# Two engines share the sums of a pairwise-tanh attention by a running tally, and last sums stay in PSUM

## The chip, the cores and the metric

The kernel runs on one core of a Trainium2 chip. The core's engines run side by side, each from its own queue, in order: TensorE (PE in the profile, its weight loads PEld), VectorE (DVE), ScalarE (ACT), GpSimd (POOL) and SyncE (SP, which issues the transfers here). Each waits on semaphores for what others made. The metric is the device time of one execution in microseconds; the median of three executions is compared. All arithmetic is fp32, and TensorE runs each fp32 matmul as two instructions.

## The reference

Two layers work on 8 images of 128 channels by 36 x 36 positions. Layer 0 normalises groups of channels, runs 3 x 3 and 1 x 1 convolutions and a softmax attention, and adds the result to x. Layer 1 takes the 1296 positions as tokens of 128 channels. Its attention scores are a sum over channels of a tanh:

```python
q = jnp.einsum('bld,ed->ble', x, Wq) + bq
k = jnp.einsum('bld,ed->ble', x, Wk) + bk
t = jnp.tanh(q[:, :, None, :] + k[:, None, :, :])
scores = jnp.einsum('bijd,d->bij', t, w) + bw[0]
attn = jax.nn.softmax(scores, axis=-1)
return jnp.einsum('bij,bjd->bid', attn, x)
```

That is 1296 x 1296 x 128 tanh values an image. After it comes a mixture of 64 experts: each expert takes its 8 best tokens of an image, weighted by a softmax over the tokens, runs a two-layer network on their weighted mean, and adds the result back to the tokens.

## The kernel before

**The scores.** The kernel never forms the tanh itself. Over a common denominator, a group of channels' tanh terms is a ratio of two sums of products of exponentials, one factor of which depends on the query alone and one on the key alone. So a numerator and a denominator are each a matmul of query features (`qf`) and key features (`kf`). A unit is one key tile (128 keys, or 16 in the last of 11 tiles) against one query chunk of 432 tokens; there are 8 images x 3 chunks x 11 tiles = 264 units. A unit has 12 slots (3 for the short last tile), 2952 in all. In each slot:

- `numerators(p)`: TensorE makes two 128 x 432 numerators into two tiles `n` of a PSUM pool of four (`ps_n`), which all other work's PSUM tiles (`aux`) take turns in too.
- `denominators(p + LAG)`, three slots ahead: TensorE makes two denominators into `d` (another pool of two), ScalarE takes Ln of them (L815), and after every second slot Exp of the negated logs (L818), which leaves reciprocals in `lq`.
- `terms(p, ns)`: VectorE multiplies each numerator by its reciprocal, and the two products join the unit's running sum.

The sum is kept in two places. In most slots the products go to an SBUF tile `rp` (pool `rpp`, three buffers, L846) and GpSimd adds both at once to `accp` (L851, L853). In the slots named by `DVE_PAIRS = (2, 5, 8, 11)`, VectorE multiplies in place in PSUM (L840) and adds each product to `accd` itself (L842; the first such slot of a unit writes `accd` by its first product, L835 to L837). At a unit's end `sums(u)` has GpSimd add the halves of `accp` and then `accd` (L860, L863), and seven slots later `exps` takes the exponential on ScalarE (L878).

**All the other work** is written as generators that stop at `yield` and are resumed between slots: `normal` (group normalisation), `conv_keys` and `layer0` (convolutions and attention of the next image), `tokens` (token normalisation of the next image), `keys`, `query_block` (query features: an Exp on ScalarE and a product by GpSimd, L594), `attend` and `gating`. `take_turns` resumes those that want no TensorE; `matmul_turn` resumes those that do, while a balance holds: each slot adds `PACE = 370` columns, and each background matmul takes its columns plus 20 off it. So the order on each engine is fixed when the program is built, by counts of slots and columns and not by time. Before the loop (up to 193 us) image 0 is prepared by the same generators without slots between; behind it (from 6240 us) the last attends, the last gating and the experts run.

**`attend`** forms the weighted token sums: 12 tiles of 108 queries an image, 96 in all. For each, two groups of matmuls over the key tiles end in two PSUM tiles `pa`. VectorE copies the first to SBUF (`sums`, L625), adds the second to it in SBUF (L628), takes the reciprocal of the last column (L630), multiplies, adds the tokens `t2` (L631) and takes statistics (L635, L636). Where a chunk of 432 is finished, the four tiles follow one another in the slots of about one and a third units.

**Layer 0's attention** forms, per chunk, ten exponentials `e`, their running total `tot` on GpSimd (L374), five pairs of matmuls `pa` that VectorE adds up in `ax` (L395, L397), then the matmul `pt` that sums `tot` over the keys, Ln and Exp of it on ScalarE (`ri`, L405, L406), and the product `ax * ri` (L412), both in SBUF.

Of the kernel before, what the change touches and what calls it, by code (L numbers as in the profile page):

```python
# [57 lines left out]
DVE_PAIRS = (2, 5, 8, 11)  # L58
# [6 lines left out]
def kernel(  # L65
# [55 lines left out]
    with ExitStack() as loop, ExitStack() as score:  # L121
# [110 lines left out]

        behind = [0]
# [9 lines left out]
        def conv_turns(taps, rows, y0, x0, width, dst):  # L243
            r0, nr = rows
            for t0 in range(0, 9, 2):
# [11 lines left out]
                if t0 == 0:  # L257
                    nc.vector.tensor_copy(dst, ps)
                else:
                    nc.vector.tensor_add(dst, ps, dst)  # L260
# [9 lines left out]
        def normal(b):  # L270
# [7 lines left out]
            for c in range(NCH):  # L278
                nc.vector.bn_stats(st[:, c, :], r[:, c * CH : (c + 1) * CH])
                yield step()  # L280
            mv = small.tile([C, 2], F32, tag="gn_mv", name="gn_mv")
            nc.vector.bn_aggr(mv, st)
# [5 lines left out]
            nc.vector.tensor_copy(gm, pm[:, :1])  # L288
            dev = small.tile([C, 1], F32, tag="dev", name="dev")
            nc.vector.tensor_sub(dev, mv[:, 0:1], gm)  # L290
            nc.vector.scalar_tensor_tensor(dev, dev, dev, mv[:, 1:2], ALU.mult, ALU.add)
# [10 lines left out]
            nc.gpsimd.tensor_scalar(wxn, wx_s, rs, None, ALU.mult)  # L302
# [5 lines left out]
            nc.vector.tensor_sub(bxn, bx_s, pb[:, :1])  # L308
            yield matmuls(1)
            for c in range(NCH):  # L310
# [3 lines left out]
                nc.vector.tensor_scalar(  # L314
# [14 lines left out]
        def layer0(b):  # L329
# [16 lines left out]
            for g in range(0, NDT, 4):  # L346
# [7 lines left out]
                nc.vector.tensor_copy(  # L354
# [3 lines left out]
                for j in range(full, len(some)):  # L358
                    n = some[j][1]
                    nc.vector.tensor_copy(vw[:n, g + j, :], tp[:n, j * C : (j + 1) * C])  # L360
                yield matmuls()
            hp = big_tile("hpre")[:, :N]
            for c in range(NCH):
# [7 lines left out]
                def total(j):  # L371
                    n = DTILES[j][1]
                    of = ex[0] if j == 1 else tot
                    nc.gpsimd.tensor_add(tot[:n], of[:n], ex[j][:n])  # L374
# [11 lines left out]
                ax = chunk_tile("ax0")  # L386
                for j0 in range(0, NDT, 2):
                    pa = aux("pa0")
                    for j in (j0, j0 + 1):
                        n = DTILES[j][1]  # L390
                        bmm(pa[:, :CH], vw[:n, j, :], ex[j][:n], start=(j == j0), stop=(j > j0))
                    yield TAKE
                    if j0 == 0:
                        total(NDT - 1)
                        nc.vector.tensor_scalar(ax, pa[:, :CH], 1.0 / D, None, ALU.mult)  # L395
                    else:
                        nc.vector.scalar_tensor_tensor(  # L397
                            ax, pa[:, :CH], 1.0 / D, ax, ALU.mult, ALU.add
                        )
                    yield matmuls()  # L400
                pt = aux("pt0")
                bmm(pt[:, :CH], ones[:DT], tot[:DT], start=True, stop=True)
                yield TAKE
                ri = chunk_tile("ri0")
                nc.scalar.activation(ri, pt[:, :CH], AF.Ln, scale=1.0 / D)  # L405
                nc.scalar.activation(ri, ri, AF.Exp, scale=-1.0)  # L406
# [742 lines left out]
```

## Time and profile before

| | |
|---|---|
| time, median of 3 runs | 6438.8 us (6434.69 to 6439.65) |
| the profiled execution: time, span | 6428.41 us, 6426.7 us |
| TensorE's mean granted clock in it | 0.966 of full speed |
| TensorE, VectorE, ScalarE, GpSimd busy | 6054.8, 4900.4, 5354.6, 4798.1 us |
| first and last VectorE product of a slot begin | 192.8 and 6236 us |
| 12 slots, ordinary unit | 23.0 us |

A row of a group reads: line, engine, operation, what it writes `<-` what it reads, shapes, count, then busy microseconds and the mean nanoseconds of one, then the engine's idle time before it and what ended that. A row of waits reads: who waited `<-` for whom, microseconds in all, how many times, the longest. TensorE's busy time counts matmuls in flight, which overlap; the idle time between them is therefore what is certainly lost, and no more than that is known from the busy share.

### The profile page before, as it was taken

What the parts mean: (1) busy time and instruction counts of PE and PEld (TensorE: products, weight loads), DVE (VectorE), ACT (ScalarE), POOL (GpSimd) and SP (SyncE); (2) the same over time, 40 slices, a digit from 0 to 9 for tenths busy, and PEclk for the clock granted to TensorE, in tenths of its full rate; (3) what the DMA queues carried; (4) which work ended last, traced back from release to release, by engine and by line L of the source; (5) the groups of instructions that cost most, each with busy time, mean ns of one, the idle gap of its engine ahead of it and who ended that gap; (6) DMA issues with size and microseconds to landing.
All of it is one profiled execution on the core that took longest, in us unless ns stands there. A gap on an engine that the chain in (4) does not pass through costs nothing.

```text
span 6426.7 us, 106771 instructions
## 1 busy us (share of the span) xinstructions
PE 6054.8 (94%) x40448; PEld 2813.9 (44%) x40448; DVE 4900.4 (76%) x9315; ACT 5354.6 (83%) x5426; POOL 4798.1 (75%) x2966
## 2 busy tenths in 40 slices
PE   8999999999999999999999999999999999999986
PEld 4444444444444444444444444444444444544432
DVE  3687778877788777888788887887778877778862
ACT  1788898888888888888888888888888888989970
POOL 3677777787777877777787787778777787888870
PEclk9999999999999999999999999999999999999997
DMA  0200011000110002100111001100011000100017
GB/s 28 66 31 23 22 63 36 30 24 27 56 46 19 24 27 68 33 26 22 44 47 38 22 23 53 43 32 25 20 63 43 23 24 27 61 26 28 24 66 253
DMA packets 155284, 265.78 MB, mean 41 GB/s; under 512 B 53712, under 2 KB 79824, under 8 KB 154768
## 3 DMA queue, kind: packets, MB, share of 16 engines
q1 hardware_dynamic: 154768, 258.95, 12.5%
q8 instruction: 318, 5.21, 0.3%
q14 instruction: 198, 1.62, 0.1%
HBM read 196.81 MB, written 61.83 MB: 40 GB/s over the span
## 4 chain that ended last, share of the span: by engine, by line
PE 67%; DVE 12%; ACT 7%; issue 7%; POOL 6%; DMA 1%; SPq 0%; POOLq 0%; DVEq 0%; ACTq 0%
PE n L793 30%; PE d L793 10%; PE pc L237 7%; PE pa L237 6%; ACT lq L815 5%; DVE n L840 3%; DVE rp L846 3%; PE s L237 3%; PE pk L237 3%; PE pq L237 2%; DVE accd L842 2%; POOL accp L853 2%; DVE t L631 1%; PE n L800 1%; POOL t L681 1%
## 5 line engine op out<-in xcount | busy, mean ns | idle before, releaser
L853 POOL TENSOR_TENSOR accp<-accp,rp 128x864 f32<-128x864 f32 x1464 | 2965.2, 2025 | 1028.0 <-DVE rp L846 975.3
L793 PE MATMUL n<-qf,kf 32*128 32x432 f32 (+1 forms) x11520 | 3239.2, 579 | 93.4 <-DVE rp L846 47.0
L815 ACT ACTIVATE lq<-d 128x864 f32<-128x864 f32 x2952 | 2552.6, 882 | 690.7 <-PE d L793 643.3
L793 PE MATMUL d<-qf,kf 32*128 32x432 f32 (+1 forms) x11520 | 2876.6, 568 | 21.2 <-ACT lq L815 16.4
L846 DVE TENSOR_TENSOR rp<-n,lq 128x432 f32<-128x432 f32 x3984 | 2202.6, 600 | 623.7 <-PE d L793 399.3
L818 ACT ACTIVATE lq<-lq 128x1728 f32<-128x1728 f32 x1488 | 2429.0, 1632 | 47.1
L793 PEld LDWEIGHTS n<-qf,kf 32*128 32x128 f32 (+1 forms) x11520 | 1167.1, 187 | 1703.4 <-DVE rp L846 586.3
L793 PEld LDWEIGHTS d<-qf,kf 32*128 32x128 f32 (+1 forms) x11520 | 1038.8, 188 | 392.2 <-issue 254.1
L840 DVE TENSOR_TENSOR n<-n,lq 128x432 f32<-128x432 f32 x1440 | 811.7, 608 | 280.1 <-PE n L793 239.2
L842 DVE TENSOR_TENSOR accd<-n,accd 128x432 f32<-128x432 f32 x1440 | 867.4, 602 | 24.7
L851 POOL TENSOR_TENSOR accp<-rp 128x864 f32<-128x864 f32 x264 | 533.8, 2022 | 221.1 <-DVE rp L846 217.5
L237 PE MATMUL pa<-xh,e 128*108 128x129 f32 x1920 | 262.6, 284 | 55.6 <-DVE rp L846 34.7
L860 POOL TENSOR_TENSOR accp<-accp 128x432 f32<-128x432 f32 x264 | 290.8, 1101 | 16.2
L237 PEld LDWEIGHTS pa<-xh,e 128*108 128x108 f32 x1920 | 223.3, 175 | 179.1 <-DVE rp L846 107.4
L594 POOL TENSOR_SCALAR qf<-qf,cs_s 128x432 f32<-128x432 f32 x192 | 262.7, 1374 | 42.0 <-ACT qf L593 42.0
L863 POOL TENSOR_TENSOR accd<-accp,accd 128x432 f32<-128x432 f32 x240 | 265.6, 1107 | 28.5 <-DVE accd L842 10.4
L237 PE MATMUL s<-q,k 128*116 128x432 f32 x480 | 229.8, 570 | 3.3 <-DVE q L260 2.1
L237 PEld LDWEIGHTS pk<-xT,a_k 128*128 128x128 f32 x1408 | 172.2, 193 | 109.8 <-DVE accd L842 27.6
L374 POOL TENSOR_TENSOR tot<-tot,e 116x432 f32<-116x432 f32 x192 | 212.0, 1104 | 6.1
L835 DVE TENSOR_TENSOR accd<-n,lq 128x432 f32<-128x432 f32 x240 | 144.9, 604 | 91.6 <-PE n L793 60.5
L381 ACT ACTIVATE e<-s 116x432 f32<-116x432 f32 x240 | 125.0, 521 | 106.6 <-PE s L237 105.5
L237 PE MATMUL pk<-xT,a_k 128*128 128x128 f32 (+1 forms) x1408 | 203.2, 288 | 2.6 <-DVE accd L842 2.3
(175 smaller groups left out, 4144.4 us busy)
## 6 DMA issues: line engine op xcount, KB each, us to landing
kf<-kd SPq DMA_DIRECT2D x240, 512.0 KB
kd<-ks SPq DMA_DIRECT2D x160, 256.0 KB
w<-in_weight_dram SPq DMA_DIRECT2D x32, 1024.0 KB
x<-in_x_dram SPq DMA_DIRECT2D x8, 648.0 KB
t<-tokd SPq DMA_DIRECT2D x96, 54.0 KB
t2d<-t2T SPq DMA_DIRECT2D x24, 216.0 KB
res<-t2d SPq DMA_DIRECT2D x8, 648.0 KB
out_dram<-res SPq DMA_DIRECT2D x8, 648.0 KB
```

Source lines behind the costliest of these rows:

```text
L237: mm(out, lhsT, rhs, **kw)
L594: nc.gpsimd.tensor_scalar(qf[:, 1, :], qf[:, 0, :], cs_s[:, q : q + 1], None, ALU.mult)
L793: mm(outs[h][:, :CH], kf[rows[h], q, :], qf_of[b, c, q][rows[h], part, :], start=True, stop=True)
L815: nc.scalar.activation(lq[:, o : o + 2, :], d[:, :, :CH], AF.Ln)
L818: nc.scalar.activation(some, some, AF.Exp, scale=-1.0)
L840: mult(ns[h], ns[h], lq[:, o + h, :])
L842: nc.vector.tensor_add(live["d"], ns[h], live["d"])
L846: mult(rp[:, h, :], ns[h], lq[:, o + h, :])
L851: nc.gpsimd.tensor_add(live["p"], live["r"], rp)
L853: nc.gpsimd.tensor_add(live["p"], live["p"], rp)
L860: nc.gpsimd.tensor_add(s[:, 0, :], s[:, 0, :], s[:, 1, :])
L863: nc.gpsimd.tensor_add(d, s[:, 0, :], d)
```

## The change

The fixed list of VectorE's slots goes. Instead two numbers, `ahead["v"]` and `ahead["g"]`, tally what has been put on VectorE and on GpSimd: a wrapper around each engine (`Tallied`) adds, for each instruction it issues, the columns of what it writes times a factor (1 for VectorE, 1.85 for GpSimd) plus a start (60 or 30). After each slot both are lowered by `SLOT = 1550`, not below 0. A slot's sum goes to VectorE when GpSimd's tally with this slot's add (3.7 x 432) would exceed VectorE's tally with its two adds, from the third slot of a unit on. Reductions and statistics count by the columns that they write; the `pow` in `rsqrt`, the slots' own products and `plus_eps` don't go through the wrapper (the products are added by hand).

In `attend` the last sum is written to the PSUM tile `pa` in place of SBUF, and reciprocal and product read it there. In `layer0` the last pair's sum is likewise written to PSUM and its product with `ri` reads it there; `pt`, Ln and Exp move ahead of the last pair; and the factor 1/D on both is dropped, since it cancels.

```diff
-DVE_PAIRS = (2, 5, 8, 11)
+SLOT = 1550
...
+        ahead = {"v": 0, "g": 0}
+
+        class Tallied:
+            def __init__(self, engine, name, by_column, start):
+                self.engine, self.name, self.cost = engine, name, (by_column, start)
+
+            def __getattr__(self, op):
+                def call(*args, **kw):
+                    dst = kw["out"] if "out" in kw else args[0]
+                    by_column, start = self.cost
+                    ahead[self.name] += by_column * dst.free_size() + start
+                    return getattr(self.engine, op)(*args, **kw)
+
+                return call
+
+        vector = Tallied(nc.vector, "v", 1, 60)
+        gpsimd = Tallied(nc.gpsimd, "g", 1.85, 30)
...
                 ax = chunk_tile("ax0")
+                ri = chunk_tile("ri0")
                 for j0 in range(0, NDT, 2):
-                    pa = aux("pa0")
+                    if j0 == NDT - 2:
+                        pt = aux("pt0")
+                        bmm(pt[:, :CH], ones[:DT], tot[:DT], start=True, stop=True)
+                        yield TAKE
+                        nc.scalar.activation(ri, pt[:, :CH], AF.Ln)
+                        nc.scalar.activation(ri, ri, AF.Exp, scale=-1.0)
+                        yield matmuls()
+                    pa = aux("pa0")[:, :CH]
...
                     if j0 == 0:
                         total(NDT - 1)
-                        nc.vector.tensor_scalar(ax, pa[:, :CH], 1.0 / D, None, ALU.mult)
+                        vector.tensor_copy(ax, pa)
+                    elif j0 < NDT - 2:
+                        vector.tensor_add(ax, pa, ax)
                     else:
-                        nc.vector.scalar_tensor_tensor(
-                            ax, pa[:, :CH], 1.0 / D, ax, ALU.mult, ALU.add
-                        )
+                        vector.tensor_add(pa, pa, ax)
+                        vector.tensor_mul(ax, pa, ri)
...
-                nc.vector.tensor_mul(ax, ax, ri)
-                nc.vector.tensor_add(hp[:, cols], px[:, :CH], ax)
+                vector.tensor_add(hp[:, cols], px[:, :CH], ax)
...
                     if j < NKT - 1:
-                        nc.vector.tensor_copy(sums, pa)
+                        vector.tensor_copy(sums, pa)
                         yield matmuls()
-                    else:
-                        nc.vector.tensor_add(sums, pa, sums)
+                vector.tensor_add(pa, pa, sums)
                 inv = small.tile([T, 1], F32, tag="inv", name="inv")
-                nc.vector.reciprocal(inv, sums[:, C : C + 1])
-                nc.vector.scalar_tensor_tensor(
-                    t2[:T, at, :], sums[:, :C], inv, t2[:T, at, :], ALU.mult, ALU.add
+                vector.reciprocal(inv, pa[:, C : C + 1])
+                vector.scalar_tensor_tensor(
+                    t2[:T, at, :], pa[:, :C], inv, t2[:T, at, :], ALU.mult, ALU.add
                 )
...
-            if k in DVE_PAIRS and not rem:
-                if k == DVE_PAIRS[0]:
+            ahead["v"] += 2 * (CH + 60)
+            if k > 1 and not rem and ahead["g"] + 3.7 * CH > ahead["v"] + 2 * (CH + 60):
+                if "d" not in live:
                     live["d"] = acc.tile([128, CH], F32, tag="accd", name="accd")
                     mult(live["d"], ns[0], lq[:, o, :])
-                    mult(ns[1], ns[1], lq[:, o + 1, :])
-                    nc.vector.tensor_add(live["d"], ns[1], live["d"])
+                    ahead["v"] -= CH + 60
+                    some = ns[1:]
                 else:
-                    for h in range(2):
-                        mult(ns[h], ns[h], lq[:, o + h, :])
-                    for h in range(2):
-                        nc.vector.tensor_add(live["d"], ns[h], live["d"])
+                    some = ns
+                for h in range(2 - len(some), 2):
+                    mult(ns[h], ns[h], lq[:, o + h, :])
+                for n in some:
+                    nc.vector.tensor_add(live["d"], n, live["d"])
+                ahead["v"] += 2 * (CH + 60)
             else:
...
-                    nc.gpsimd.tensor_add(live["p"], live["r"], rp)
+                    gpsimd.tensor_add(live["p"], live["r"], rp)
                 else:
-                    nc.gpsimd.tensor_add(live["p"], live["p"], rp)
+                    gpsimd.tensor_add(live["p"], live["p"], rp)
+            for name in ahead:
+                ahead[name] = max(ahead[name] - SLOT, 0)
...
             if units[u][2] < NKT - 1:
+                if "d" not in live:
+                    return s[:, 0, :]
                 d = live.pop("d")
```

Everywhere else `nc.vector` and `nc.gpsimd` become the wrappers `vector` and `gpsimd`, with the same instructions.

## The prediction

> **What bounds the kernel now.** I read the page first (busy shares, slices, the chain of waits), then stretches of the main loop one unit long (a unit is one key tile against one query chunk, 12 slots), then the groups by line, last what PE waited for. Busy shares and the chain:
>
> ```profile
> PE 6054.8 (94%) x40448; PEld 2813.9 (44%) x40448; DVE 4900.4 (76%) x9315; ACT 5354.6 (83%) x5426; POOL 4798.1 (75%) x2966
> ...
> PE 67%; DVE 12%; ACT 7%; issue 7%; POOL 6%; DMA 1%; SPq 0%; POOLq 0%; DVEq 0%; ACTq 0%
> PE n L793 30%; PE d L793 10%; PE pc L237 7%; PE pa L237 6%; ACT lq L815 5%; DVE n L840 3%; DVE rp L846 3%; PE s L237 3%; PE pk L237 3%; PE pq L237 2%; DVE accd L842 2%; POOL accp L853 2%; DVE t L631 1%; PE n L800 1%; POOL t L681 1%
> ```
>
> No engine is idle enough to be free, and PE leads. The stretches say where that differs: the loop; an ordinary unit; one in which three attend tiles finish; one in which new query blocks are made; one just after a token normalisation.
>
> ```profile
> 300.00:6200.00 5900.00, 5652.69 (x38212) 2603.81 (x38210) 4686.91 (x8889) 5171.72 (x5214) 4605.05 (x2814) 0.98 0.11 34
> 1882.20:1905.20 23.00, 22.92 (x120) 10.06 (x119) 19.93 (x38) 20.49 (x20) 17.43 (x10) 1.00 0.09 24
> 2001.00:2025.90 24.90, 22.83 (x155) 12.72 (x153) 23.25 (x50) 21.19 (x20) 16.99 (x10) 1.00 0.06 18
> 2152.80:2179.00 26.20, 26.07 (x118) 9.94 (x119) 18.01 (x33) 24.21 (x29) 24.59 (x18) 1.00 0.05 12
> 2387.20:2412.40 25.20, 21.88 (x116) 10.08 (x109) 18.43 (x34) 20.43 (x20) 24.81 (x21) 0.86 0.08 24
> ```
>
> After the length come PE, PEld, DVE, ACT and POOL busy time. In the ordinary unit PE is busy 22.92 of 23.0 us: nothing taken from DVE can shorten it. With attends, DVE is at 23.25 of 24.9 and PE stands idle for 2.07. With query blocks PE (26.07 of 26.2) and ACT are full. After a normalisation POOL is full (24.81 of 25.2) and PE loses 3.3. In all, PE is idle for 5900 - 5653 = 247 us of the loop, and no more can be won there.
>
> ```profile
> L853 POOL TENSOR_TENSOR accp<-accp,rp 128x864 f32<-128x864 f32 x1464 | 2965.2, 2025 | 1028.0 <-DVE rp L846 975.3 <-DVE vw L360 2.1 <-DVE nm L709 1.5
> ...
> L846 DVE TENSOR_TENSOR rp<-n,lq 128x432 f32<-128x432 f32 x3984 | 2202.6, 600 | 623.7 <-PE d L793 399.3 <-POOL accp L851 78.1 <-PE n L793 51.2
> ...
> L842 DVE TENSOR_TENSOR accd<-n,accd 128x432 f32<-128x432 f32 x1440 | 867.4, 602 | 24.7
> ...
> L631 DVE SCALAR_TENSOR_TENSOR t<-sums,inv,t 108x128 f32<-108x128 f32 x96 | 87.9, 915 | 29.0 <-DMA t<-tokd 25.7
> ...
> L628 DVE TENSOR_TENSOR sums<-pa,sums 108x129 f32<-108x129 f32 x96 | 28.0, 292 | 18.2 <-PE pa L237 17.4
> ```
>
> A slot whose sum stays on DVE costs it two products (600 to 608 ns each) and two adds (602); one handed to POOL costs DVE two products and POOL one add of 2025. DVE also waited 78.1 us for POOL to free an rp buffer. What PE itself waited for in the loop, and the chain inside the attend stretch:
>
> ```profile
> PE n L793 <- DVE rp L846: 47.0, 26, 7.9
> PE pa L237 <- DVE rp L846: 34.7, 45, 1.2
> PE n L793 <- DVE accd L842: 23.4, 27, 2.6
> ...
> PE pa L237 <- DVE accd L842: 10.9, 27, 0.8
> ```
>
> ```profile
> by line: PE pa L237 24.5%; PE n L793 15.4%; DVE t L631 14.2%; DVE rp L846 11.4%; DVE n L840 8.2%; issue 4.7%; DVE accd L842 4.3%; DVE t_st L635 3.7%; DVE sums L628 3.5%; PE d L793 2.5%; DVE accd L835 2.4%; PE pc L237 2.4%; DVE inv L630 2.1%
> ```
>
> DVE ended about 161 of the 231 us that all rows of that view of PE's waits add up to. In the attend stretch the one product t (L631) is 14.2% of 24.9 us, 3.5 us for three tiles.
>
> **The change, part by part.** *Who adds.* The built programs' instruction orders give the tally's choices: adds into accd fall from 1680 to 1098, POOL's adds of a whole slot rise from 1464 to 1755. Each of 240 units has one first DVE slot with one add; so 240 + 2 x 429 = 1098 means 669 DVE slots in place of 960. DVE loses 582 x 0.602 = 350 us, POOL gains 291 x 2.025 = 589. The usual unit (116 of 240) has 2 DVE slots for 4; units with query blocks have 6 (41 of them).
>
> - Ordinary unit: DVE 19.93 - 4 adds x 0.602 = 17.5; POOL 17.43 + 2 x 2.025 = 21.5; PE stays at 22.92. Worth 0, as long as POOL at 21.5 of 23 stays covered by PE.
> - Query blocks: POOL 24.59 - 2 x 2.025 = 20.5, DVE 18.01 + 4 x 0.602 = 20.4; PE at 26.07 covers both. Worth 0.
> - Outside the attends, PE's waits ended by adds into accd (54 us over all its rows) shrink with the DVE slots, by 30%: -16.
>
> *Attends.* The last sum is written back to PSUM and the product reads it there. The sum keeps its 292 ns. The product takes 350/674/1841 ns (minimum, median, maximum) with both tensors in SBUF; with one in PSUM the nearest rows are L628 of the same shape (292) and the same operation out of PSUM at 432 columns (L397, 608, against 602 for an add of that shape, so the operation itself costs no more). Bounds: 292 and 674; I take 300, nearest to L628. So 96 x 0.615 = 59 us less DVE. With three tiles in the attend stretch DVE falls to 23.25 - 4 x 0.602 - 3 x 0.615 = 19.0, below PE's 22.83; what is late next is PE. The 96 tiles make 32 such stretches: 32 x 2.07 = -66 if all PE idle time goes. The PSUM tile is held longer, over the reciprocal (164) and the product, 0.46 us a tile, 45 us in all if PE waited for each; but the next slot's products stand behind these instructions on DVE anyway, and the four n buffers turn over before PE wants that one: 0. SP issues the same transfers.
>
> *Layer 0.* Its last product reads PSUM instead of SBUF: 24 x (816 - 607) = 5 us of DVE, hidden. The matmul of the softmax totals moves ahead of the last pair of pa, so PE may now stand before POOL's last total (1.10 us). Bounds: 0, or one POOL add each time, 24 x 2.0 = 49. Four pa groups of 904 columns at a pace of 370 a slot lie between, some 8 slots: 0. In the three chunks done before the loop, Ln and Exp (0.52 and 0.56) slip beside the last pa: -3. The last attends behind the loop: -2.
>
> *What POOL's longer queue costs.* No row shows POOL this full over a long time. From below 0: in the new order as many slot adds precede the token normalisation's end as before. From above, the two added adds of each unit after a normalisation (two per batch, 16) land on a full POOL: 16 x 4.05 = 65. I take +13, a fifth, nearer to the order listing.
>
> Sum: -16 - 66 - 3 - 2 + 13 = -74. The chain gives a check: (3% + 2%) of 6427 over 960 DVE slots is 0.335 us each, 3% over 1992 POOL slots 0.097; 291 x 0.238 = -69, the product 64 x 0.67 = -43, POOL 129 / 1464 x 291 = +26: -86. The profiled execution took 6428.4 (span 6426.7), 10.4 below the median 6438.8. 6428.4 - 74 + 10.4 = 6365.
>
> **A rule that speaks against it.** POOL takes 2025 ns for what DVE does in 1204, 1.68 times as long, so engine time rises by 239 us. The Trainium skill (GPSIMD Engine Reference, 4.1 Engine selection) puts elementwise two-input work on VectorE because GpSimd is about 2x slower; as an estimate by that page the moved adds would cost POOL 291 x 2.41 = 701 us, and whoever holds to it expects a loss. The row decides: 1.68, on the engine with the most idle time.
>
> **Rivals.**
> - *POOL becomes late* (slower). For: 21.5 of 23 us in ordinary units, and the tally prices a 128-column normalisation at 267 columns where a slot add's 2025 ns stand for 1598, so 0.34 us for a measured 0.79, and eleven or twelve in a row leave 5 us uncounted; the third rp buffer then blocks DVE, as it did for 4.46 us in the last stretch. Against: only 82 us of such waits now, and POOL is idle 1295 us of the loop. A quarter of an add lost in each of 240 units is +120: 6485. It decides from 0.31 us a unit on.
> - *PE hides it* (no change). For: 22.92 of 23.0. Only the product pays, -43, and POOL takes +26 back: 6422; with a little more from POOL, 6438. The tally counts columns, not time, so it may also miss the moments that matter.
> - *All waits on DVE go.* -161: 6278. For: DVE falls under PE in every kind of unit. Against: much of it is products that stay.
>
> **How the numbers follow.** Forecast 0.50, POOL late 0.22, PE hides it 0.14, all waits 0.14. 0.2% (13 us) is about what a measurement can tell from no change: faster 0.50 + 0.14 + 0.06 = 0.70, same 0.08, slower 0.22. Range 6275 (all waits) to 6480 (most of the first rival); the forecast alone 6315 to 6410.
>
> **What would show it.** Right: DVE busy near 4490, POOL near 5390, the t product near 300 ns, attend stretches under 23.5 us, ordinary units still 23. Wrong: rp's wait for POOL well over 150 us, POOL without idle time through several units, or attend stretches as long as before.

## The result and the profile after

The changed kernel took 6495.7 us (median of 4 runs, 6484.7 to 6498.2) against 6436.7 for the kernel before on the same chip: ratio 1.009, 95% interval 1.0073 to 1.0108. It is slower by 59 us between these medians, 58 by the ratio; the forecast was 6365, the range 6275 to 6480. The profiled execution took 6484.7 us, its span is 6483.0.

Busy time and the chain of waits on the page of the kernel after:

```profile
PE 6139.5 (95%) x40448; PEld 2883.2 (44%) x40448; DVE 4531.4 (70%) x8733; ACT 5369.7 (83%) x5426; POOL 5383.9 (83%) x3257
...
PE 73%; POOL 9%; DVE 6%; issue 5%; ACT 5%; DMA 1%; SPq 0%; POOLq 0%; DVEq 0%; ACTq 0%
```

VectorE (DVE) gave up 369 us of work (forecast 350 + 59) and its share of the chain halved (12% to 6%); GpSimd (POOL) took 586 us and its share rose from 6% to 9%. TensorE (PE) is busy 85 us longer with the same 40448 matmuls. So they ran slower. The stretches that answer those shown of before (the loop; the ordinary unit; the attend unit; the unit that the prediction named after its query blocks; the unit after the token normalisation, each window cut near the first product of the unit), in the table by windows of the kernel after (length, then busy PE, PEld, DVE, ACT and POOL, the granted clock, and two columns on DMA):

```profile
300.00:6200.00 5900.00, 5688.73 (x38006) 2646.58 (x38001) 4291.56 (x8263) 5143.20 (x5172) 5130.59 (x3072) 0.97 0.11 34
1883.60:1907.70 24.10, 23.66 (x126) 10.05 (x130) 18.38 (x34) 20.95 (x20) 22.98 (x14) 1.00 0.12 39
2001.40:2025.90 24.50, 24.40 (x158) 14.10 (x161) 19.40 (x45) 20.40 (x19) 21.23 (x13) 1.00 0.13 44
2156.90:2184.00 27.10, 26.79 (x128) 11.12 (x124) 20.67 (x38) 23.75 (x26) 18.86 (x15) 1.00 0.07 20
2391.00:2425.20 34.20, 29.34 (x135) 13.27 (x132) 16.45 (x30) 22.50 (x23) 30.76 (x24) 0.75 0.11 34
```

The ordinary unit went from 23.0 to 24.1 us. The fourth went from 26.1 to 26.7 us between first products (the window shown is 0.4 us wider) with VectorE busier by 2.7 (in the kernel before GpSimd's rows there are nine of layer 0's totals, `tot`, and no query feature, so the prediction's name for it was wrong); the unit after the token normalisation from 25.2 to 34.2, at a mean clock of 0.75 instead of 0.86. TensorE's idle time in the 300 to 6200 us stretch fell, from 247 to 211 us; over the whole loop, the same work in both, from 251 to 226. What VectorE waited for (whole span), and what TensorE waited for in the loop:

```profile
DVE rp L869 <- POOL accp L246: 231.1, 147, 4.9
```

```profile
PE n L813 <- DVE rp L869: 79.5, 67, 3.6
...
PE n L813 <- DVE accd L864: 15.7, 39, 0.7
```

The wait for GpSimd tripled (78.1 before), one of the signs named for a wrong forecast. Another, GpSimd without idle time through several units, showed as well: its longest stretch without a gap over 0.2 us is 110 us, near the end of the loop, against 36 before. These waits are not where most of the time went, as the experiments show.

To place the time, the units of an image are counted 0 to 32 in the order they run (5, 16 and 27 are the short ones), and their lengths are summed over the eight images. *Gate* is units 2 and 3, where the gate's tokens are normalised; *token* is 26 to 29, from layer 0's Tanh to the token normalisation of the next image; *attend* is 0, 1, 11, 12, 22, 23; *full* is 10, 21, 32 (seven query features each on GpSimd) and 15, 19, 24 (some four to nine of layer 0's totals). The last column is the time that the trace's clock records show TensorE at half its clock within the loop. The first row is in us, the others are differences from it, from one profiled execution each.

| kernel | gate | token | full | attend | other units | half clock |
|---|---|---|---|---|---|---|
| before, us | 405 | 698 | 1214 | 1174 | 2553 | 303 |
| after | +25 | +34 | +30 | -53 | +18 | 430 |
| e1, attends only | +6 | -12 | -6 | -45 | +4 | 285 |
| e2, tally only | +6 | -7 | +43 | -18 | +4 | 321 |
| e5, layer 0 only | +18 | +40 | -14 | -4 | +24 | 408 |
| e12, pause only | +17 | +56 | -17 | -4 | +43 | 450 |
| e13, layer 0, late | +3 | -9 | -22 | +12 | +11 | 278 |
| e14, whole change, late | +5 | -18 | +29 | -66 | +11 | 260 |
| e15, e1 and e13 | +7 | -12 | -23 | -34 | +10 | 296 |
| e21, e14 with old slots in *full* | +10 | -9 | -20 | -40 | +8 | 299 |

So most of the forecast attend gain came, and the losses outweighed it: gate, token and full units above all.

### The profile page after: what moved, and what is told of

It is laid out like the page before. It is cut to its first block, busy times and chain, and to the rows that moved or that the text cites. A ratio compares the mean times of both kernels' runs of the same rounds, so it can differ in the third digit from the quotient of the medians.

```text
span 6483.0 us, 106890 instructions
## 1 busy us (share of the span) xinstructions
PE 6139.5 (95%) x40448; PEld 2883.2 (44%) x40448; DVE 4531.4 (70%) x8733; ACT 5369.7 (83%) x5426; POOL 5383.9 (83%) x3257
## 4 chain that ended last, share of the span: by engine, by line
PE 73%; POOL 9%; DVE 6%; issue 5%; ACT 5%; DMA 1%; SPq 0%; POOLq 0%; DVEq 0%; ACTq 0%
PE n L813 33%; PE d L813 12%; PE pc L257 7%; PE pa L257 7%; POOL accp L246 6%; PE s L257 3%; ACT lq L835 3%; PE pk L257 3%; PE pq L257 2%; DVE rp L869 2%; DVE n L862 1%; PE d L820 1%; PE n L820 1%; POOL xh L246 1%; DVE accd L864 1%
## 5 line engine op out<-in xcount | busy, mean ns | idle before, releaser
L246 POOL TENSOR_TENSOR accp<-accp,rp 128x864 f32<-128x864 f32 x1755 | 3551.2, 2023 | 691.9 <-DVE rp L869 581.0
L813 PE MATMUL n<-qf,kf 32*128 32x432 f32 (+1 forms) x11520 | 3300.4, 583 | 135.4 <-DVE rp L869 86.8
L869 DVE TENSOR_TENSOR rp<-n,lq 128x432 f32<-128x432 f32 x4566 | 2517.9, 600 | 1060.5 <-PE d L813 503.2
L813 PE MATMUL d<-qf,kf 32*128 32x432 f32 (+1 forms) x11520 | 3007.5, 572 | 37.4 <-ACT lq L835 32.6
L813 PEld LDWEIGHTS n<-qf,kf 32*128 32x128 f32 (+1 forms) x11520 | 1193.6, 188 | 1776.2 <-DVE rp L869 717.2
L813 PEld LDWEIGHTS d<-qf,kf 32*128 32x128 f32 (+1 forms) x11520 | 1104.7, 189 | 397.8 <-issue 238.1
L862 DVE TENSOR_TENSOR n<-n,lq 128x432 f32<-128x432 f32 x1098 | 630.5, 609 | 226.8 <-PE d L813 104.7
L864 DVE TENSOR_TENSOR accd<-n,accd 128x432 f32<-128x432 f32 x1098 | 662.3, 603 | 22.9
L246 POOL TENSOR_TENSOR accp<-rp 128x864 f32<-128x864 f32 x264 | 533.5, 2021 | 25.3 <-DVE rp L869 24.1
L246 POOL TENSOR_TENSOR accp<-accp 128x432 f32<-128x432 f32 (+2 forms) x312 | 316.6, 1015 | 21.6
L257 PE MATMUL pa<-e,vw 116*128 116x432 f32 x480 | 203.1, 549 | 6.0 <-DVE accd L864 5.7
```

The costliest lines, as they stand in the source:

```text
L246: return getattr(self.engine, op)(*args, **kw)
L257: mm(out, lhsT, rhs, **kw)
L813: mm(outs[h][:, :CH], kf[rows[h], q, :], qf_of[b, c, q][rows[h], part, :], start=True, stop=True)
L862: mult(ns[h], ns[h], lq[:, o + h, :])
L864: nc.vector.tensor_add(live["d"], n, live["d"])
L869: mult(rp[:, h, :], ns[h], lq[:, o + h, :])
```

## The experiments

Ratios are to the kernel before on the same chip, with 95% intervals; its medians there lay between 6426.9 and 6436.7 us. Gains and losses in us are worked out from the ratios where nothing else is said. Theory A said: the tally puts adds onto GpSimd where it also normalises, VectorE and then TensorE stand there, and the attend edit is a gain by itself. B: moved load costs everywhere. C: holding the attend tile in PSUM costs. L and I: the layer 0 edit costs by itself, or only together with the tally.

### The three edits one at a time

**e1_attend_psum**: the kernel before with the attend edit.

```diff
-                    else:
-                        nc.vector.tensor_add(sums, pa, sums)
+                nc.vector.tensor_add(pa, pa, sums)
...
-                nc.vector.reciprocal(inv, sums[:, C : C + 1])
+                nc.vector.reciprocal(inv, pa[:, C : C + 1])
```

> The kernel before with one edit alone: in attend the last sum is written to the PSUM tile and the product reads it there. Theory A (the changed kernel loses because GpSimd comes late where the token and gate normalisations fall on a queue that the tally has filled; the attend edit is a real gain): the product falls from 915 to about 350 ns, the attend stretches lose their idle PE time, 40 to 66 us in all, ratio to before 0.990 to 0.994. Rival C (the longer hold of the PSUM tiles costs TensorE more than the shorter product saves): ratio 1.000 or above. Rival B (the moved adds cost everywhere, since GpSimd is 1.68 times as slow) says nothing on this run.

Measured 6377.4 us, 0.9913 (0.9898 to 0.9928). C falls. From the groups by line, the product in e1:

```profile
L630 DVE SCALAR_TENSOR_TENSOR t<-pa,inv,t 108x128 f32<-108x128 f32 x96 | 33.7, 351 | 27.5 <-DMA t<-tokd 24.2
```

915 ns became 351, and its spread went from 350-1841 to 349-354 ns. The two traces show why. In the kernel before, 56 of the 96 products took over 600 ns; each began while a GpSimd add ran and ended 146 to 153 ns after that add did. The 16 that began with GpSimd idle took 350 to 353, and so did the 24 that met the last 125 ns of an add. In e1, 67 of the 96 lie wholly within a GpSimd instruction and take 349 to 354 all the same. The saving of 56 us is the attend term of the forecast (66) less a sixth.

**e2_tally_only**: the change without its attend and layer 0 edits (both parts as in the kernel before).

> The changed kernel with the attend and the layer 0 edits undone, so the tally alone. Theory A: the loss of the changed kernel without the attends' gain, 59 + 55 = about 115 us, ratio 1.014 to 1.021; VectorE's waits for an rp buffer at about 230 us, as in the changed kernel. Rival C: the tally is harmless and the run is at 1.000 to 1.004.

Measured 6467.5 us, 1.005 (1.0035 to 1.0065): a loss of 32 us, a good deal less than the 115 that A wanted. The waits of VectorE for GpSimd came to 180.9 us.

**e5_layer0_alone**: the kernel before with the layer 0 edit (totals' matmul ahead of the last pair, last sum and product in PSUM, no pause after `ri`).

> The kernel before with the layer 0 edit alone (the totals' matmul, Ln and Exp ahead of the last pair of pa; last sum and product out of PSUM), fixed VectorE slots, attend as before. The attend edit alone gave 0.9913 and the tally alone 1.005, so the whole change should have been at 0.996 and was at 1.009: about 84 us are left for this edit or for its meeting with the tally. Theory L (the edit costs by itself, TensorE standing before the totals or PSUM tiles held longer): 1.008 to 1.014. Theory I (it only shifts the background work by a few slots, and the tally's choices then meet the token normalisation badly): 0.997 to 1.003.

Measured 6493.7 us, 1.0095 (1.0076 to 1.0113). The edit costed at nothing costs 61 us, more than the whole change's 58. L holds.

**e9_tally_attend**: the change without its layer 0 edit.

> The changed kernel with the layer 0 edit alone undone: tally and attend edit. If the parts add up, 1.005 x 0.9913 = 0.996, 6410 us. Theory L and theory I both expect 0.993 to 0.999; a value near 1.009 would mean that the tally and the attend edit are at odds by themselves, and the layer 0 edit is innocent.

Measured 6400.9 us, 0.9952 (0.9936 to 0.9968): e1 and e2 multiply to 0.9963. Adding -56, +32 and +61 gives +37, so some 20 us of the 58 are the parts acting together.

### Waits for GpSimd that can be removed without gain

**e3_true_prices** and **e10_prices_no_layer0**: the tally with measured durations instead of columns for normalisations, the power, statistics, `max` and reciprocals, in the whole change and without the layer 0 edit.

```diff
+        PRICES = {
+            "v": {"bn_stats": 213, "bn_aggr": 146, "max": 1190, "reciprocal": 131},
+            "g": {"tensor_scalar": (1.5, 435), "tensor_tensor": (0, 1750)},
+        }
...
-            nc.gpsimd.tensor_tensor(dst, ve, neg_half[:p, :f], ALU.pow)
+            gpsimd.tensor_tensor(dst, ve, neg_half[:p, :f], ALU.pow)
```

> The changed kernel with the tally's prices put right by measured durations: a GpSimd normalisation of 128 columns at 627 instead of 267, the power at 1750 instead of nothing, VectorE's statistics at 213 and 146 instead of 66 and 62. The programs' order shows 1972 whole-slot adds on GpSimd instead of 2019, and two fewer in the two units after a token normalisation. Theory A: the stall there shrinks by about 4 us of 10 an image and 2 us at the gate normalisation, 30 to 65 us in all, ratio to before 0.999 to 1.005, waits for an rp buffer under 170 us. Rival B: the share moved is nearly the same, so 1.007 to 1.011 stays.

> The same as the last (tally and attend edit, layer 0 as before), with the measured prices in the tally. In the changed kernel the prices took 57 us out of the loop, 10.4 us an image from the unit after the token normalisation and 4.5 from the one after the gate normalisation. With layer 0 as before the stretch after the token normalisation costs only 0.7 us an image more than in the kernel before, so theory I expects less from the prices here: 0.988 to 0.996. Theory L expects the full 57 us again: 0.985 to 0.988.

Measured 0.9982 (0.9972 to 0.9992) and 0.9947 (0.9928 to 0.9966). In the whole change the prices win back some 70 us. In the profiled executions the loop is 57 us shorter: the token units give back 56 and the gate units 26, and the other units grow by 25. Without the layer 0 edit they are worth nothing that can be told from zero, although VectorE waits 42 us less for GpSimd (138.9 against 181.1). So the mispriced normalisations were seen to matter only where layer 0's edit has moved them.

**e7_norms_on_vector**: the whole change, with both normalisations (`xh` and `t2`) on VectorE.

> The changed kernel with the token and gate normalisations (23 an image, 0.79 us each on GpSimd) issued on VectorE. The tally then puts 2060 whole-slot adds on GpSimd instead of 2019. Theory A: the long runs of normalisations are what makes GpSimd late, so the stretches after a normalisation come back to about 25 us, the waits for an rp buffer fall under 100 us and the ratio to before is 0.985 to 0.997. Rival B: GpSimd still carries 1.68 times the moved work, and more of it: 1.005 or above. A third possibility is that these products, with their operands in SBUF, wait on VectorE for GpSimd as the product of attend did (674 to 1841 ns): then VectorE is late in their place.

Measured 1.0097 (1.008 to 1.0114): no gain, though from the view of waits

```profile
DVE rp L869 <- POOL accp L246: 155.9, 140, 2.6
```

a third of the wait is gone. VectorE was late instead, the third possibility: the normalisations took 1.04 and 1.23 us there, 0.79 on GpSimd, and the unit with the token normalisation grew by 11.6 us while the next shrank by 11.1 (images 1 to 6). So e7 moves the delay and does not decide on A by itself. As the account of the 58 us A falls by e2, with 32 us instead of 115, and by e5, which costs 61 without any tally.

**e11_attend_three_pairs**: e1 with `DVE_PAIRS = (2, 6, 10)`, that is 1968 pair adds on GpSimd, spread evenly, against about 2020 by the tally and 1728 before.

> The attend edit with three fixed VectorE slots a unit, 2, 6 and 10, instead of four: 240 more whole-slot adds on GpSimd (1968 of them, nearly as many as the tally gives), spread evenly and with no tally. If the moved load itself costs (theory B), this is slower than the attend edit alone (0.9913): 0.996 to 1.004, with more wait for an rp buffer in every kind of unit, most of all where query blocks are made, since GpSimd there was at 24.6 of 26.2 us and gets 2 more. If the load moved is harmless and only its placing by the tally costs, 0.987 to 0.993.

Measured 1.0177 (1.0161 to 1.0192), 170 us above e1. A regular list that moves as much as the tally does far worse, and nearly everywhere: the other units alone are 63 us longer than in e1. That speaks for B, but this list also gives GpSimd three slots in a row where the old one gave two, and the run does not tell the two apart. Moved load as such need not cost: e21 below has 339 adds more on GpSimd than e1 and takes the same time.

### Layer 0: the edit, or the slot it ends in

In the order of the instructions the layer 0 edit moves every background step behind it: layer 0's output 2 to 3 slots earlier, the token variances from slot 28.7 (unit 28, slot 7) to 28.4, the gate's variances from 2.0 to 1.11 (in images 2 to 6; up to one slot less in the first two). What does that is the pause of one slot after `ri`, which the edit drops.

**e12_rest_only**: the kernel before without that pause, and nothing else.

```diff
                 nc.scalar.activation(ri, ri, AF.Exp, scale=-1.0)
-                yield matmuls(1)
+                yield matmuls()
```

> The kernel before with one thing changed: layer 0's pause of one slot after ri's two activations is gone (matmuls(1) becomes matmuls()), as the change also has it. Counted from the order of the instructions, every background step then lands in exactly the slots that the layer 0 edit alone gave it: layer 0's output 2 to 3 slots earlier, the token normalisation 3, the gate 1. Theory S (shift): the layer 0 edit costs 1.0095 only because the background work behind it meets the slots elsewhere; then this is 1.007 to 1.012, with the units 26, 29 and 3 of an image longer by 3 to 7 us. Theory H (hold): what costs is the last sum and product in PSUM, or TensorE standing before GpSimd's last total now that pt comes ahead of the last pair; then this is 0.999 to 1.002.

**e13_layer0_late**: the layer 0 edit, with two slots of pause added ahead of the Tanh.

```diff
-            yield step(2)
+            yield step(4)
             nc.scalar.activation(hp, hp, AF.Tanh, bias=hb)
```

> The layer 0 edit alone (which took 1.0095), with two more slots of pause ahead of the Tanh (step(2) becomes step(4)). Counted from the order of the instructions, layer 0's output, the tokens and the gate are back in exactly the slots they had before; layer 0's own chunks stay up to 3 slots early. Theory S: 0.996 to 1.001, the edit's own saving being a few us and the rest gone with the shift. Theory H: 1.007 to 1.012, since the hold in PSUM and the early pt are all still there.

**e14_after_late** and **e15_attend_layer0_late**: the same line in the whole change, and in e1 with the layer 0 edit.

> The whole change with the same two slots of pause ahead of the Tanh. Token normalisation and gate lie in the slots of the kernel before. Theory S: 0.990 to 0.997, the place of tally and attends without the layer 0 edit (0.9952) less at most some 25 us. Theory H: 1.005 to 1.010, near the whole change's 1.009.

> The kernel before with the attends' edit and the layer 0 edit, the old pairs (no tally), and the two slots of pause ahead of the Tanh. Theory S: 0.987 to 0.993, the attends' 0.9913 or a little under; below 0.9913 it is the fastest of all. Theory H: 0.999 to 1.003, 0.9913 times 1.0095.

**e18_layer0_one_later**: e13 with `step(3)`.

> The layer 0 edit alone with one slot of pause ahead of the Tanh in place of two: the token normalisation is 2 slots earlier than in the kernel before, the gate 1 earlier, as it was with the edit alone. Shifts of 3 and 1 took 1.0095, of 0 and 0 took 0.9992. If the cost grows with the distance, 1.003 to 1.008. If it is one event that turns over at a place (the gate's variances landing in the last slot of unit 1 instead of the first of unit 2), 1.008 to 1.012 or, where the token part carries it, 0.999 to 1.004.

| kernel | output, tokens, gate earlier by (slots) | ratio |
|---|---|---|
| e12 | 3, 3, 1 | 1.0151 (1.0134 to 1.0168) |
| e5 | 3, 3, 1 | 1.0095 (1.0076 to 1.0113) |
| e18 | 2, 2, 1 | 1.009 (1.0075 to 1.0105) |
| e13 | 0, 0, 0 | 0.9992 (0.9983 to 1.0002) |
| e14 | 0, 0, 0 | 0.996 (0.9945 to 0.9974) |
| e15 | 0, 0, 0 | 0.9919 (0.9904 to 0.9934) |

Theory S is right in e13, e14 and e15, and in e12 by its sign, the cost lying above its range; H is wrong in all four. One pause dropped costs 97 us by itself, although not one instruction is added; one line that puts the later steps back into their slots takes 6495.7 to 6406.1. The rest of the edit (PSUM, and the earlier totals' matmul) is worth 36 us at the moved place (1.0151 to 1.0095) and hardly to be told from nothing at the old one (0.9992, an interval up to 1.0002). The cost doesn't grow with the distance: two slots cost what three do. Both the gate units and the token units are longer in e18 (+21 and +26 us). Image 1 tells the two apart in part: its gate stands at 1.11 in the kernel before too, and its token steps move by 2 slots (in e18 by 1). Its token units are still 9 us longer in e5 and e12, and 6 in e18, so the token steps cost without the gate's.

What happens there: units 26 and 29 of one image, by windows, in the kernel before, then in e12, then in e13, where both are back at their old length.

```profile
2326.00:2353.40 27.40, 23.94 (x344) 11.36 (x338) 19.52 (x36) 25.94 (x25) 17.93 (x11) 0.94 0.06 20
...
2387.20:2412.40 25.20, 21.88 (x116) 10.08 (x109) 18.43 (x34) 20.43 (x20) 24.81 (x21) 0.86 0.08 24
```

```profile
2340.60:2376.00 35.40, 32.11 (x344) 13.98 (x338) 21.40 (x36) 25.60 (x25) 17.03 (x12) 0.71 0.05 15
...
2408.30:2441.10 32.80, 27.22 (x132) 12.82 (x131) 18.92 (x36) 22.36 (x24) 25.59 (x19) 0.79 0.10 35
```

```profile
2327.70:2355.20 27.50, 24.22 (x344) 11.40 (x344) 19.50 (x36) 25.93 (x25) 18.37 (x11) 0.94 0.09 29
...
2393.50:2418.70 25.20, 21.80 (x116) 10.10 (x111) 18.42 (x34) 20.45 (x20) 24.81 (x21) 0.86 0.08 24
```

In unit 26 of e12 the same 344 matmuls take 8.2 us more of TensorE, at 0.71 of the clock. What came ahead of the slow stretches, from e12's timeline of TensorE (start, duration, and in brackets the idle time before):

```profile
2349.93 0.63 PE L793 MATMUL n<-qf,kf 64*128 64x432 f32 x1 [1.41 <-DVE hpre L413]
2357.73 1.46 PE L793 MATMUL d<-qf,kf 64*128 64x432 f32 x4 [1.86 <-ACT lq L815]
```

Two stalls, 1.41 us behind the last chunk's sum on VectorE and 1.86 us behind the two table loads and the Tanh on ScalarE. After the first the clock record shows 3.4 us at half, after the second 17.1 us. With the pause these two came in other slots: in the kernel before, the unit has one stall of 3.12 us and 3.4 us at half clock. So a longer stall is not always followed by a longer half-clock piece. In the unit after the token normalisation, VectorE's wait for an `rp` buffer in the kernel before, and in e12:

```profile
2397.09 1.12 DVE L846 TENSOR_TENSOR rp<-n,lq 128x432 f32<-128x432 f32 x2 [4.46 <-POOL accp L851]
```

```profile
2421.40 1.12 DVE L846 TENSOR_TENSOR rp<-n,lq 128x432 f32<-128x432 f32 x2 [6.37 <-POOL accp L851]
```

1.9 us more. TensorE's stall behind it goes from 2.90 to 5.58 us and the half clock from 6.8 to 13.7 us; the unit is 7.6 us longer. In the whole change that unit holds three such waits:

```profile
2395.53 1.12 DVE L869 TENSOR_TENSOR rp<-n,lq 128x432 f32<-128x432 f32 x2 [3.43 <-POOL accp L246]
2400.60 1.12 DVE L869 TENSOR_TENSOR rp<-n,lq 128x432 f32<-128x432 f32 x2 [2.27 <-POOL accp L246]
2407.23 1.12 DVE L869 TENSOR_TENSOR rp<-n,lq 128x432 f32<-128x432 f32 x2 [4.92 <-POOL accp L246]
```

with 17.1 us at half clock. Over the loop the change runs 127 us more at half clock (430 against 303). Half of that, some 64 us, is an estimate of the full-speed work lost by it: about the whole loss, while TensorE's idle time fell.

### What the tally costs

With the places restored the tally still costs some 25 us (e9 against e1, e14 against e15). In the table its loss is in the *full* units, 51 us between e15 and e14, against 33 won in the attend units. There it gives VectorE up to six slots, some next to each other, where the old list gave four, three apart. Of the 110 pairs of neighbouring VectorE slots in e14, 74 stand in the full units.

**e16_at_most_four** and **e17_as_many_adds**: e14 with VectorE capped at four slots a unit, and e14 with GpSimd's side of the comparison raised.

```diff
+            if (k > 1 and not rem and on_v.get(u, 0) < 4
+                    and ahead["g"] + 3.7 * CH > ahead["v"] + 2 * (CH + 60)):
```

```diff
+            if k > 1 and not rem and ahead["g"] + 3.7 * CH + 260 > ahead["v"] + 2 * (CH + 60):
```

> The whole change with the two slots of pause (which took 0.996), and VectorE's part in a unit capped at four slots, as many as the kernel before gives it. In six units of an image (10, 15, 19, 21, 24 and 32) the tally had given VectorE five or six, and those were 0.7 to 1.3 us longer than with the old fixed slots. Theory P (place): the tally loses what it loses in those six units, about 50 us over the images, and gains in the others; then this is 0.986 to 0.993. Theory M (moved load): an add on GpSimd costs wherever it stands; this kernel has 2046 of them for the pairs against 1728 before, so it is 0.995 to 1.001, the same as without the cap or worse.

> The whole change with the two slots of pause, and 260 columns added to GpSimd's side of the tally's comparison, so that GpSimd gets 1780 adds of the pairs instead of about 2020 (1728 in the kernel before). VectorE's part in units 10, 15, 19, 21 and 32 stays six or seven slots. Theory M: with the moved load gone the tally costs nothing, 0.988 to 0.9925, the attends and layer 0 late with the old slots having taken 0.9919. Theory P: the six units are still long and the others lose part of their gain, 0.996 to 1.003.

Measured 1.0006 (0.9997 to 1.0016) and 1.0 (0.999 to 1.0011). Each kept one theory and broke the other: fewer VectorE slots in the full units did not help, and fewer adds on GpSimd did not either. Both make more of VectorE's slots stand next to each other: 152 and 149 against 110 in e14.

**e19_never_two_running** and **e20_two_running**: e14 with `k - on_v.get(u, -9) >= 2` as a further condition, and e15 with `DVE_PAIRS = (2, 5, 6, 11)`. (Of the six units that these expectations speak of, three have query features and three layer 0's totals.)

> The whole change with the two slots of pause, and a condition added to the tally: VectorE never takes two slots running. GpSimd gets 2053 adds of the pairs (2019 without the condition), VectorE 635 slots (670). Theory R (running): in the traces three slots VectorE, GpSimd, GpSimd took 2.57, 1.04 and 2.50 us with the old slots, and VectorE, VectorE, GpSimd 2.50, 2.19 and 1.98 with the tally, 0.56 us more; the tally makes 110 such pairs of slots, the cap of four 152, the 260 columns 149, and by 0.56 us each the two should take 22 us more than without, and took 23. So without any this is 0.984 to 0.991, the fastest yet. Theory M (moved load): 2053 adds on GpSimd, and more of them queued in the six units with query features; like the cap of four, 0.998 to 1.003.

> The attends and layer 0 late with fixed slots (which took 0.9919), VectorE's slots in a unit being 2, 5, 6 and 11 in place of 2, 5, 8 and 11: as many adds on each engine, in each unit, and one pair of slots running in each of 240 units. Theory R: 240 times 0.56 us is 134 us more, 1.005 to 1.018. Theory M: nothing is moved between the engines, so 0.989 to 0.996.

Measured 1.0022 (1.0012 to 1.0031) and 1.0159 (1.0144 to 1.0174). e20 bears R out: with not one add moved between the engines, 240 neighbouring slots cost 155 us, 0.65 each. Between the starts of the products, slot 6, the new neighbour, is 0.81 us longer on average and the other eleven together 0.24 shorter. TensorE's wait for VectorE's adds, in e15 and then in e20:

```profile
PE n L793 <- DVE accd L842: 23.2, 26, 2.6
```

```profile
PE n L793 <- DVE accd L842: 45.8, 63, 2.3
```

The list of e20 also gives GpSimd four slots in a row (7 to 10) instead of two. That rival does not show: those four slots together took no longer, and VectorE's main wait for GpSimd did not grow, in e15 and then in e20:

```profile
DVE rp L846 <- POOL accp L851: 79.8, 30, 8.8
```

```profile
DVE rp L846 <- POOL accp L851: 75.2, 24, 7.7
```

A pair costs in every kind of unit: 0.44 us in the full ones, 0.53 in the other ones, 0.84 in the token units.

e19 refutes R's forecast. The token units grow by 47 us over e14 and the half clock from 260 to 379 us. And without a single neighbouring pair the full units still took 1239 us, where e14 took 1242 and e15, with the old list, 1191. There the tally now puts VectorE's slots two apart, and three slots VectorE, GpSimd, VectorE took 6.94 us on average, as long as VectorE, VectorE, GpSimd in e14 (6.96), against 6.26 for VectorE, GpSimd, GpSimd in e15. So what costs there is not the neighbour alone; slots two apart took as long. Nor is it their number alone: under the cap of four (e16) the full units took 1231 us.

**e21_old_slots_in_six**: e14 with the old list in the full units.

```diff
+            if k > 1 and not rem and (
+                k in OLD if u % 33 in FULL
+                else ahead["g"] + 3.7 * CH > ahead["v"] + 2 * (CH + 60)
+            ):
```

> The whole change with the two slots of pause (0.996), and in the units 10, 15, 19, 21, 24 and 32 of an image VectorE's slots are the old 2, 5, 8 and 11 whatever the tally says; it decides everywhere else. In these units GpSimd has seven query features or nine of layer 0's totals besides, ScalarE is full (1191 us busy over all of them in both kernels), and with the tally they took 51 us more in all, ScalarE standing idle 93 us instead of 62. Theory Q (full units): VectorE's slots next to each other delay TensorE's next denominators, and only where ScalarE is full nothing makes it up again; with the old slots there the 51 us come back and the 33 us that the tally wins in the attend units stay: 0.986 to 0.992, level with or under the fastest so far (0.9919). Theory M (moved load): GpSimd gets 2067 adds of the pairs, as many as under the cap of four (2046, 1.0006), and its queue spills into the units behind: 0.997 to 1.003.

Measured 6376.6 us, 0.9918 (0.9904 to 0.9932), though GpSimd has 2067 pair adds, more than in e14. Q's forecast holds, at the edge of its range: the full units come back (1193 us against 1242), but 27 of the 33 us won in the attend units go. That the loss lay in these units because ScalarE is full there is not shown: in e20 a pair cost no more there than elsewhere, and most of the tally's pairs stand there. ScalarE is busy 23.7 of 25.8 us in unit 10 of one image of e15. Its waits there, in e15, e14 and e21:

```profile
ACT lq L815 <- PE d L793: 1.0, 1, 1.0
```

```profile
ACT lq L835 <- PE d L813: 2.9, 4, 1.4
```

```profile
ACT lq L836 <- PE d L814: 1.0, 1, 1.0
```

A VectorE slot holds its two `n` buffers until its adds are done; three slots VectorE, GpSimd, GpSimd took 2.57, 1.04 and 2.50 us in e15, VectorE, VectorE, GpSimd 2.50, 2.19 and 1.98 in e14, and the whole unit 25.8 and 27.0 us (27.0 in e19, with no neighbours). TensorE issues the next `d` behind `n`, and ScalarE waits for `d`. Over all full units ScalarE is busy 1112 us in e15, 1122 in e14 and 1113 in e21, and idle 79, 120 and 80 (the 1191 us of the expectation add up durations that overlap).

The fastest versions are e1 (6377.4), e15 (6377.1) and e21 (6376.6): the attend edit alone gives all of it.

## Why the prediction was wrong

- **The attends, -66: nearly right.** -56 alone; the product took 351 ns where 300 was taken, and TensorE's idle time over the loop fell from 251 to 200 us in e1. What had it slow was its SBUF operands: the Trainium skill (SBUF — State Buffer, SBUF: two separate sides) says that a VectorE operation with two SBUF inputs contends for one shared pair of ports with a GpSimd operation that reads SBUF, and that the loser is blocked for all of the other's instruction. The traces agree: the 56 slow products each ended about 150 ns after the GpSimd add that ran when they began, and with one tensor in PSUM none was slow.
- **Layer 0, "0": the step that failed.** It cost 61 us (e5). Both bounds (0 and 49) were for TensorE standing before GpSimd's last total (four groups at 370 columns a slot are 9.8 slots, not 8, but nothing hangs on it). The cost was not there: e13 keeps the early totals' matmul and costs nothing, and e12, which drops the pause alone, costs 97 us. The prediction followed the instructions that were edited, not the ones that come after in the same queue of background steps: it missed `matmuls(1)` becoming `matmuls()`. Comparing slot numbers of `x`, `ve` and `nm` in the two instruction orders would have shown 3, 3 and 1 slots, though not the price, which was mostly half clock (303 us before, 408 in e5).
- **"Query blocks: ... Worth 0": the second** (the stretch read for it was one of layer 0's totals, the working the same). The tally cost between 43 and 51 us there in the profiled executions (e2 against before, e14 against e15). TensorE and ScalarE were both called full, and that was taken as cover; a later `n` was a loss there, not hidden.
- **-16 and +13 for the rest of the tally:** the whole tally came to +25 (e9, e14) to +32 us (e2); outside the full units it was worth about -15 to -40 in the profiled executions. The chain check (-86) shared the mistake: it priced a slot by its mean share, not by which slots stand beside it.
- **Head -3, tail -2:** the stretches before and after the loop grew by 2 us together.
- **The sum treats stalls as what they last.** Every term counted TensorE's idle microseconds, of which 247 were called all that could be won. For the attends that served. For the moved steps it did not: e12 has 11 us more of idle time over the loop than the kernel before and 147 more at half clock, and its loop is 95 us longer.
- **The rule that speaks against it** was right in direction for an even list: 240 adds more on GpSimd cost 170 us (e11 against e1, with longer runs of GpSimd slots too). It was not for e21, where 339 more cost nothing. The row's ratio held (2023 ns against two times 603, 1.68).
- **The rivals.** "POOL becomes late" gave 6485, near the result, and its sign showed (231 us). But e7 and e10 cut that wait by 75 and 42 us without gain; lateness counted only where the shift had put it. That nearness is no confirmation.
- **Signs that came true:** DVE 4531 (near 4490), POOL 5384 (5390), four of the six attend units under 23.5 us on average over images 1 to 6 (22.0 to 23.0; the other two 24.0 and 24.5). They say that the edit did what it says, not what it costs. Ordinary units did not all stay at 23: the one shown went to 24.1.

Left open: why a shift of one or two slots costs about as much as one of three, the 20 us that the parts cost only together, and why VectorE slots two apart lose in the full units.

## What to carry to other kernels

Where background work is laid into a main loop by a schedule, any edit that adds or drops a yield moves everything behind it; compare the slot of every later step, and put back the old place with a pause before judging the edit itself (here 6495.7 became 6406.1 with one line). When load is balanced between two engines, look at where the heavy slots stand and not only at their number: here two neighbouring ones cost 0.4 us or more in every kind of unit. Measure each part of a change alone: here one part carried all of the gain.

## What the runs showed of the hardware

The granted clock has only two values in these records, 1.0 and 0.5, in pieces that nearly all are multiples of 3.4 us. The Trainium skill (TensorE: Matmul & The Clock Gate, Part 1) states both, and names an idle window of about 3.4 us as what brings the lower one. The first agrees; here shorter idle times were enough. In the loops of before, after and e12 together, of 75 idle gaps of TensorE of 2 us or more, 67 were met by a half-clock piece that began within the gap or 3.5 us after it; of 71 gaps of 1.2 to 2 us, 44; of 383 gaps of 0.4 to 1.2 us, 51. A stall of 1.86 us was followed by 17.1 us at half clock, with no idle time over 0.2 us in the 18 us after it. What ends a half-clock piece was not tried, and no run here changed a stall alone.

A kernel can thus have less idle time on TensorE and still be slower: over the loop 226 us against 251, with 127 us more at half clock.
